# An image network of four layers on one core: the last queries' features in parts behind the key products, keys' values in two banks, shared reciprocals, last taps mixed later, lone steps reordered

## The chip, the cores and the metric

The kernel runs on one core of a Trainium2 chip, in one launch, all in fp32. The metric is the device time of one execution in microseconds (us). Before the change three executions took 2716.63, 2718.47 and 2719.44 us; the median, 2718.47 us, is the time before.

A core has a matrix engine (TensorE, PE in the profile; its weight loads are PEld), a vector engine (VectorE, DVE), a scalar engine (ScalarE, ACT), a general one (GpSimd, POOL) and queues for transfers (SP issues them here). [...] this kernel makes three buffers of two banks ("pair") and two single banks[...]. [...]

## The reference, cut to what matters

x has the shape (4, 512, 64, 64): four images, 512 channels, 4096 pixels. Four layers follow each other, image by image.

```python
# layer 0: attention over the pixels, 64 features
attn = softmax(einsum('bdk,bdq->bkq', key_, query), axis=1)
x = scale * einsum('oc,bchw->bohw', w_out, value @ attn) + x
# layer 1: three convolutions (1x1, 3x3, 1x1); kernels mixed from 8 experts by
# rw = sigmoid(mean over pixels of x @ router_w.T + router_b)
x = relu(bn(conv3(relu(bn(conv2(relu(bn(conv1(x)))))))) + x)
# layer 2: linear attention
Q, K = softplus(Wq x + bq), softplus(Wk x + bk)      # 64 features each
V = Wv x + bv
KV = einsum('bmn,bcn->bmc', K, V)
norm = 1.0 / einsum('bnm,bm->bn', Q, K.sum(-1) + EPS)
x = x + gamma * einsum('bnm,bmc,bn->bcn', Q, KV, norm)
# layer 3: a gate of discounted sums along the columns and then the rows
g = w_proj x + b_proj                                # 1024 channels: gates and sums
x = x + gamma * g[:512] * sigmoid(ds_cumsum_rows(ds_cumsum_columns(g[512:])))
```

## The kernel before, as far as the change touches it

An image is held in four tiles `xs[pr]` of 1024 pixels ("pairs" of two 512-pixel blocks). The order on TensorE is that of the program. `manual_schedule(DVE)` fixes VectorE's order too; elsewhere the order on VectorE and ScalarE is chosen when the program is built.

```python
def pair_psum(name):
    return ps.tile([P, 2, NB], F32, tag="s", name=name, bufs=3)
def bank(name, shape=(P, NB)):
    return ps.tile(list(shape), F32, tag="acc", name=name)
# ... cut ...
def four(name):
    return fourp.tile([P, 2, NB], F32, tag="four", name=name)
# ... cut ...
def mix_by_expert(wc, rw, experts):
    _, j, n, ex = experts
    to = wc[:, j:j + n, :]
    nc.vector.tensor_scalar(to, ex[:, :, 0, :], rw[:, 0:1], None, ALU.mult)
    for e in range(1, E):
        nc.vector.scalar_tensor_tensor(to, ex[:, :, e, :], rw[:, e:e + 1], to, ALU.mult, ALU.add)
```

The end of layer 0: the residual sums of the last two pairs, with the mixing of the experts' kernels (`mix`: on TensorE; `mix_by_expert`: on VectorE, for the last three taps).

```python
for m in range(2, KC):
    out_before(m)
ys = [out_product(pr, m) for m in range(3)]
add_out(pr, 0, ys[0])
mix(wcq, sel, ex0)
ys.append(out_product(pr, 3))
for m in range(1, KC):
    add_out(pr, m, ys[m])
for m in range(KC):
    xm = xs[pr - 1][:, m, :]
    nc.vector.tensor_tensor(xm, xm, flat(ring[8 + m]), ALU.add)
sum_range(pr)
# ... cut ...
mix(wc, sel, ex4)
mix(wc, sel, ex7)
mix_by_expert(wc, rw, ex10)
```

Layer 2: features (two softplus halves per pair of pairs), transposes of the keys and of x, and the sum of key products `g`, which is folded and multiplied with the value weights instead of making V.

```python
def softplus(w, pair, z):
    i = 2 * (len(kts) // 2 % 2)
    e, u = sp[:, i], sp[:, i + 1]
    pos, ln = four(f"pos_{b}_{w}_{pair[0]}"), four(f"ln_{b}_{w}_{pair[0]}")
    nc.scalar.activation(e, z, AF.Abs, bias=col(BQ2 + w))
    nc.scalar.activation(pos, z, AF.Relu, bias=col(BQ2 + w))
    nc.scalar.activation(e, e, AF.Exp, scale=-1.0)
    nc.vector.tensor_scalar(u, e, 1.0, None, ALU.add)
    nc.scalar.activation(ln, u, AF.Ln)
    return lambda: softplus_end(w, pair, e, u, pos, ln)
def softplus_end(w, pair, e, u, pos, ln):
    nc.vector.scalar_tensor_tensor(u, u, -1.0, e, ALU.add, ALU.subtract)
    nc.vector.tensor_tensor(pos, pos, ln, ALU.add)
    for i, pr in enumerate(pair):
        if w:
            k = block(f"k_{b}_{pr}")
            nc.vector.scalar_tensor_tensor(k, pos[:, i, :], 1.0, u[:, i, :], ALU.mult, ALU.subtract,
                                           accum_out=ks[:, pr:pr + 1])
            kts[w, pr] = k
        else:
            nc.vector.tensor_tensor(qs[:, pr, :], pos[:, i, :], u[:, i, :], ALU.subtract)
            kts[w, pr] = None
# ... cut ...
def move(pr, j):
    xtr = pair_psum(f"xtr_{b}_{pr}_{j}")
    for h in range(2):
        n0 = h * NB + j * P
        for kc in range(KC):
            nc.tensor.transpose(xtr[:, h, kc * P:(kc + 1) * P], xs[pr][:, kc, n0:n0 + P], ident)
    xt = four(f"xt_{b}_{pr}_{j}")
    (nc.scalar.copy if j % 2 or (pr > 1 and j) else nc.vector.tensor_copy)(xt, xtr)
    moved.append(xt)
# ... cut ...
h2[2] = conv2(2)
conv3(1, h2[1])
h2[3] = conv2(3)
weights = load_quarters(b)
features(1, (0, 1))()()
conv3(2, h2[2])
rest = features(0, (0, 1))
with tc.manual_schedule(engines={mybir.EngineType.DVE}):
    key_transpose((0, 1))
    rest()()
for step in ahead(0):
    step()
conv3(3, h2[3])
products(0, ahead(1))
weights[2]()
features(1, (2, 3))()()
products(1, ahead(2))
rest = features(0, (2, 3))
# ... cut ...
def normed(pr, between=None):
    den = bank(f"den2_{b}_{pr}")
    nc.tensor.matmul(den, kbd, qs[:, pr, :], start=True, stop=True)
    nrm = block(f"nrm_{b}_{pr}")
    nc.vector.reciprocal(nrm, den)
    if between:
        between()
    nc.vector.tensor_tensor(qs[:, pr, :], qs[:, pr, :], nrm, ALU.mult)
# ... cut ...
def value_product(pr, m):
    y = pair_psum(f"wv_{b}_{pr}_{m}")
    for h in range(2):
        r = slice(h * D, (h + 1) * D)
        nc.tensor.matmul(y[:, h, :], kv[r, m * P:(m + 1) * P], qs[r, pr, :], start=True, stop=True)
    return y
def value_add(pr, m, y):
    xm = xs[pr][:, m, :]
    nc.vector.tensor_tensor(xm, flat(y), xm, ALU.add)
return value_product, value_add, weights, wcq
```

Layer 3: each block takes seven products (a saving of one in eight against the plain form) for two channel groups of a pair. `s` steps make the sums, `g` steps the gates of the block before, `l` the scans of the block before, `y` and `a` a value product of layer 2 and its addition to x. `x` is one single bank of a block, `zy` one pair.

```python
def product(self, k):
    if k == 1:
        self.x = bank(f"sx_{self.name}")
        self.zy = pair_psum(f"zy_{self.name}")
    y = self.x if k in (1, 6, 7, 4) else self.zy[:, 0 if k == 2 else 1, :]
    w, v = weights[k], others[self.pr][k]
    for c in range(2):
        nc.tensor.matmul(y, w[:, c, self.kind, self.j * P:(self.j + 1) * P], v[:, c, :],
                         start=c == 0 and k in (1, 5), stop=c == 1,
                         skip_group_check=k not in (1, 5))
def seed(self):
    nc.scalar.copy(self.zy[:, 0, :], self.x)
def copy_out(self, k):
    self.e[k] = block(f"e{k}_{self.name}")
    nc.scalar.activation(self.e[k], self.x, AF.Identity, bias=self.bias[k - 2])
# ... cut ...
tiles = [(pr, (pr + j) % 2) for pr in range(NPAIR) for j in range(2)]
units = {}
steps = (("s1", "s seed", "l rows 1"), ("g1", "g seed", "y", "l rows 0", "l turn 1"),
         ("s5", "l turn 0", "a"), ("g5", "l columns 1"),
# ... cut ...
last_steps = (("g1", "g seed", "l rows 1", "l rows 0"), ("g5",), ("g6", "g copy_out 2", "l turn 1"), ("g2",),
              ("g7", "g copy_out 3", "l columns 1", "g fourth", "l turn 0", "l columns 0", "l sigmoid 1",
               "l sigmoid 0"), ("g4",), ("g3", "g third", "g first", "g second"))
# ... cut ...
with tc.manual_schedule(engines={mybir.EngineType.DVE, mybir.EngineType.Activation}):
    for m in range(KC):
        value_add(0, m, value_product(0, m))
        if m == 1:
            sum_x(0, 0)
    for part in range(1, 4):
        sum_x(0, part)
# ... cut ...
for i in range(len(tiles) + 1):
    who = {"l": last, "s": Sums(1, i) if i < len(tiles) else None, "g": Gates(0, i - 1) if i else None}
    made = None
    for step in steps if who["s"] else last_steps:
        for what in step:
            name, *args = what.split()
```

## Time and profile before

| what | before |
|---|---|
| time, median of 3 | 2718.47 us |
| span of the profiled execution | 2717.1 us |
| TensorE busy | 2667.3 us (98%) |
| VectorE busy | 1961.2 us (72%) |
| ScalarE busy | 1306.6 us (48%) |
| moved by DMA | 115.15 MB, mean 42 GB/s |
| reciprocals of layer 2 (VectorE, 128 x 512) | 16, 3356 ns each |
| clock granted to TensorE | 0.997 |

Busy time is a union of instructions[...]. [...] A wait in the profile is idle time of an engine, with the instruction whose end released it. Line numbers (L588) are those of the kernel before.

### The profile page before, as it was taken

To read this page: it belongs to the slowest core of one execution; us is meant where nothing else is said; L and a number is where in the kernel's file an instruction comes from. 1 tells how busy PE (TensorE), PEld (TensorE's weight loads), DVE (VectorE), ACT (ScalarE), POOL (GpSimd) and SP (SyncE) were. 2 spreads that over 40 slices of the span, in tenths; PEclk is the share of its full clock that TensorE was granted. 3 is DMA by queue.
4 is the path that set the end of the run, shared out by engine and by line. 5 is a ranking of instruction groups with operands and counts; after the bars stand their busy time and mean duration, and the time that the engine had idled before them with its cause. 6 is when DMAs were issued, how large, how long until landed. Compare 5 with 4: busy or idle time off the path is not lost.

```text
span 2717.1 us, 25649 instructions
## 1 busy us (share of the span) xinstructions
PE 2667.3 (98%) x10046; PEld 1114.7 (41%) x10046; DVE 1961.2 (72%) x2197; ACT 1306.6 (48%) x1483; POOL 10.7 (0%) x26
## 2 busy tenths in 40 slices
PE   8999999999999999999999999999999999999998
PEld 3333364344333345444433334544443333554443
DVE  2688766787468876678747778667874777866787
ACT  4544354445555535345555453535555555352545
POOL 1000000000000000000000000000000000000000
PEclk9999999999999999999999999999999999999999
DMA  5000200021200020002220002001121000200011
GB/s 188 1 1 0 101 31 1 16 108 74 82 1 1 1 101 31 1 24 101 78 78 1 1 1 101 32 0 60 64 108 47 1 1 1 101 31 1 31 47 48
DMA packets 34545, 115.15 MB, mean 42 GB/s; under 512 B 2928, under 2 KB 12144, under 8 KB 32880
## 3 DMA queue, kind: packets, MB, share of 16 engines
q1 hardware_dynamic: 34416, 113.43, 11.1%
q8 instruction: 81, 1.33, 0.2%
q14 instruction: 48, 0.39, 0.0%
HBM read 79.86 MB, written 33.55 MB: 42 GB/s over the span
## 4 chain that ended last, share of the span: by engine, by line
PE 86%; DVE 9%; ACT 2%; DMA 1%; issue 1%; SPq 1%; DVEq 0%; ACTq 0%
PE s L248 17%; PE av L263 17%; PE sx L769 14%; PE zy L769 11%; PE c L444 4%; PE kq L209 4%; PE c L493 3%; PE c L516 2%; PE z L543 2%; PE wv L687 2%; PE vv L209 2%; PE g L605 2%; PE xtr L588 2%; PE c2e L493 2%; PE y L307 1%
## 5 line engine op out<-in xcount | busy, mean ns | idle before, releaser
L248 PE MATMUL s<-qv,key 64*128 64x512 f32 x2048 | 469.1, 603 | 1.8 <-ACT ring L251 1.8
L256 DVE TENSOR_TENSOR acc<-acc,ring 128x1024 f32<-128x1024 f32 x312 | 381.7, 1223 | 100.7 <-ACT ring L251 71.9
L251 ACT ACTIVATE ring<-s 128x1024 f32<-128x1024 f32 x336 | 317.7, 1038 | 224.1 <-PE s L248 224.0
L263 PE MATMUL av<-ring,qv 128*64 128x512 f32 x1344 | 304.5, 595 | 0.0
L248 PEld LDWEIGHTS s<-qv,key 64*128 64x128 f32 x2048 | 189.4, 187 | 274.8 <-issue 173.2
L256 DVE TENSOR_TENSOR acc<-acc,ringx 128x1024 f32<-128x1024 f32 x168 | 205.5, 1223 | 102.8 <-ACT ringx L251 90.2
L251 ACT ACTIVATE ringx<-s 128x1024 f32<-128x1024 f32 x176 | 172.1, 1040 | 207.0 <-PE s L248 207.0
L769 PE MATMUL sx<-t,sx 128*128 128x512 f32 x512 | 236.9, 597 | 0.0
L263 PEld LDWEIGHTS av<-ring,qv 128*64 128x64 f32 x1344 | 93.3, 137 | 198.6 <-issue 198.6
L263 PE MATMUL av<-ringx,qv 128*64 128x512 f32 x704 | 167.2, 598 | 0.0
L774 ACT COPY zy<-sx 128x512 f32<-128x512 f32 x64 | 36.5, 570 | 240.1 <-PE sx L769 230.6
L819 DVE TENSOR_TENSOR_SCAN t<-sx,t 128x512 f32<-128x512 f32 x128 | 148.8, 1210 | 1.7
L769 PEld LDWEIGHTS sx<-t,sx 128*128 128x128 f32 x512 | 95.9, 190 | 127.8 <-issue 121.1
L808 ACT COPY t<-s 128x1024 f32<-128x1024 f32 x64 | 127.2, 1994 | 40.5 <-DVE s L802 40.5
L778 ACT ACTIVATE e<-sx,prm_sb 128x512 f32<-128x512 f32 x128 | 86.9, 686 | 123.8 <-PE sx L769 123.8
L802 DVE TENSOR_TENSOR_SCAN s<-wc,s 128x512 f32<-128x512 f32 x128 | 146.0, 1204 | 0.0
L825 ACT ACTIVATE s<-t 128x1024 f32<-128x1024 f32 x64 | 125.5, 1987 | 1.0 <-DVE t L819 0.9
L769 PE MATMUL sx<-t,wq 128*128 128x512 f32 x256 | 117.0, 598 | 7.5 <-ACT e L778 7.5
L209 PE MATMUL kq<-x,wqkv_sb 128*64 128x512 f32 x512 | 116.2, 607 | 6.3 <-DMA x<-in_x_dram 5.6
L769 PE MATMUL zy<-t,wq 128*128 128x512 f32 x256 | 118.7, 604 | 2.5 <-ACT zy L774 2.5
L769 PE MATMUL zy<-x,wq 128*128 128x512 f32 x256 | 116.2, 594 | 0.0
L769 PE MATMUL sx<-x,wq 128*128 128x512 f32 x256 | 116.2, 594 | 0.0
(195 smaller groups left out, 3390.0 us busy)
## 6 DMA issues: line engine op xcount, KB each, us to landing
out_dram<-s SPq DMA_DIRECT2D x64, 512.0 KB, 2.6
x<-in_x_dram SPq DMA_DIRECT2D x15, 2048.0 KB, 8.5
ex<-in_packed_dram SPq DMA_DIRECT2D x8, 1536.0 KB, 6.3
ex<-in_packed_dram SPq DMA_DIRECT2D x4, 2048.0 KB, 7.9
ex<-in_experts_dram SPq DMA_DIRECT2D x4, 2048.0 KB, 7.9
wq<-in_wproj_t_dram SPq DMA_DIRECT2D x32, 256.0 KB, 4.5
ex<-in_experts_dram SPq DMA_DIRECT2D x4, 1536.0 KB, 7.1
x<-in_x_dram SPq DMA_DIRECT2D x4, 512.0 KB, 6.3
```

The lines of the kernel that those rows point to most:

```text
L209: nc.tensor.matmul(y[h * D:(h + 1) * D, :], wqkv_sb[:, kc, col0:col0 + D], xs[pr][:, kc, h * NB:(h + 1) * NB], start=kc == 0, stop=kc == K ...
L248: nc.tensor.matmul(s[:, h, :], key[r, kt * P:(kt + 1) * P], qry[r, pr * NB:(pr + 1) * NB], start=True, stop=True)
L251: nc.scalar.activation(p, s, AF.Exp)
L256: nc.vector.tensor_tensor(accs[pr], accs[pr], p, ALU.add)
L263: nc.tensor.matmul(avs[pr][h * D:(h + 1) * D, :], vt[:, kt, :], ring[i % RING][:, h, :], start=kt == 0, stop=kt == NT - 1)
L444: nc.tensor.matmul(y[:, h, :], wc[:, kc, :], xs[pr][:, kc, h * NB:(h + 1) * NB], start=kc == 0, stop=kc == KC - 1)
L493: nc.tensor.matmul(y[:, lo - a:hi - a], u, v[:, lo:hi], start=dy == 1, stop=dy == 2)
L769: nc.tensor.matmul(y, w[:, c, self.kind, self.j * P:(self.j + 1) * P], v[:, c, :], start=c == 0 and k in (1, 5), stop=c == 1, skip_group_c ...
L802: nc.vector.tensor_tensor_scan(self.half(i, h), along[:, self.j + 2 * i, :], self.half(i, h), 0.0, ALU.mult, ALU.add)
L808: nc.scalar.copy(self.t[i].rearrange("p (w r) -> p w r", w=W), self.s[i].rearrange("p (r w) -> p w r", w=W))
L819: nc.vector.tensor_tensor_scan(th, down[:, i, :], th, 0.0, ALU.mult, ALU.add)
L825: nc.scalar.activation(self.s[i].rearrange("p (r w) -> p w r", w=W), tw, AF.Sigmoid)
```

## The change

It has five parts. The features of the last two pairs' queries leave the middle of layer 2: their products come in four parts, behind the key products, between the folding steps and the value products, and in the first block of layer 3; their softplus and division follow in the first two blocks. The product of keys and values goes into two single banks of 256 columns. The denominators of two pairs are made with 16 equal columns per head instead of 64, so that two pairs share one reciprocal of 64 rows, and a small product (`spread`) sends the inverse back to all rows. The last taps are mixed behind the last residual sums. And single steps change their order: the second transpose of x goes through single banks, transposes and key products alternate in twos instead of ones, VectorE's order is fixed in the whole middle of layer 2, and the first and last block of layer 3 have orders of their own.

```diff
+    kbd = const.tile([P, 32], F32, tag="kbd", name="kbd")
     nc.gpsimd.memset(kbd, 0.0)
+    spread = const.tile([P, P], F32, tag="spread", name="spread")
+    for h in range(2):
+        nc.vector.tensor_reduce(spread[:, h * D:h * D + 1], ident.rearrange("p (q i) -> p i q", i=32)[:, 16 * h:16 * h + 1, :],
+                                AX.X, ALU.add)
+        nc.vector.tensor_scalar(spread[:, h * D:(h + 1) * D], ones[:, 0:D], spread[:, h * D:h * D + 1], None, ALU.mult)
... cut ...
             for m in range(1, KC):
                 add_out(pr, m, ys[m])
+            mix_by_expert(wcq, rw, ex10)
             for m in range(KC):
... cut ...
         mix(wc, sel, ex7)
-        mix_by_expert(wc, rw, ex10)
... cut ...
+        def move_by_halves(pr, j):
+
+            xt = four(f"xt_{b}_{pr}_{j}")
+            for h in range(2):
+                n0 = h * NB + j * P
+                xtr = bank(f"xtr_{b}_{pr}_{j}_{h}")
+                for kc in range(KC):
+                    nc.tensor.transpose(xtr[:, kc * P:(kc + 1) * P], xs[pr][:, kc, n0:n0 + P], ident)
+                nc.scalar.copy(xt[:, h, :], xtr)
+            moved.append(xt)
... cut ...
         def products(pr, between=()):
-            between = list(between)
-            for j in range(TPB):
-                t = pr * TPB + j
-                if j + 2 < TPB:
-                    move(pr, j + 2)
-                elif between:
-                    between.pop(0)()
-                xt = moved.pop(0)
-                for h in range(2):
-                    nc.tensor.matmul(g[h * D:(h + 1) * D, :], kts[pr][:, j, h * D:(h + 1) * D], xt[:, h, :],
-                                     start=t == 0, stop=t == NPAIR * TPB - 1)
+            for j0 in range(0, TPB, 2):
+                for step in [lambda j=j: move(pr, j) for j in (2, 3)] if j0 == 0 else between:
+                    step()
+                for j in range(j0, j0 + 2):
+                    t = pr * TPB + j
+                    xt = moved.pop(0)
+                    for h in range(2):
+                        nc.tensor.matmul(g[h * D:(h + 1) * D, :], kts[pr][:, j, h * D:(h + 1) * D], xt[:, h, :],
+                                         start=t == 0, stop=t == NPAIR * TPB - 1)
... cut ...
+        def invert(pair):
+            den = bank(f"den2_{b}_{pair[0]}")
+            for i, pr in enumerate(pair):
+                nc.tensor.matmul(den[32 * i:32 * (i + 1), :], kbd, qs[:, pr, :], start=True, stop=True,
+                                 tile_position=(0, 32 * i))
+            inv = block(f"inv_{b}_{pair[0]}")
+            nc.vector.reciprocal(inv[0:D, :], den[0:D, :])
+            return inv
+
+        def divide(pair, inv):
+            nrm = pair_psum(f"nrm_{b}_{pair[0]}")
+            for i, pr in enumerate(pair):
+                r = slice(32 * i, 32 * (i + 1))
+                nc.tensor.matmul(nrm[:, i, :], spread[r, :], inv[r, :], start=True, stop=True,
+                                 tile_position=(32 * i, 0))
+            q = qs[:, pair[0]:pair[1] + 1, :]
+            nc.vector.tensor_tensor(q, q, nrm, ALU.mult)
... cut ...
-            rest()()
-        for step in ahead(0):
-            step()
-        conv3(3, h2[3])
-        products(0, ahead(1))
-        weights[2]()
-        features(1, (2, 3))()()
-        products(1, ahead(2))
-        rest = features(0, (2, 3))
... cut ...
-        with tc.manual_schedule(engines={mybir.EngineType.DVE}):
+            rest = rest()
+            move(0, 0)
+            move_by_halves(0, 1)
+            conv3(3, h2[3])
+            g = bank(f"g_{b}", (P, C))
+            keys = features(1, (2, 3))
+            rest()
+            keys = keys()
+            products(0, ahead(1))
+            keys()
+            products(1, ahead(2))
... cut ...
-                nc.vector.tensor_scalar(kbd[r, r], ones[r, 0:D], ksum[r, :], 1e-6, ALU.mult, ALU.add)
+                nc.vector.tensor_scalar(kbd[r, 16 * h:16 * (h + 1)], ones[r, 0:16], ksum[r, :], 1e-6, ALU.mult, ALU.add)
             key_transpose((2, 3))
-            rest = rest()
-            normed(0)
-            rest()
-        products(2, ahead(3))
-
-        normed(1)
-        products(3, [lambda: normed(2)])
-        g_sb = block(f"gsb_{b}", (P, C))
-        nc.scalar.copy(g_sb, g)
... cut ...
-        def make_kv():
+            inv = invert((0, 1))
+            products(2, ahead(3))
+            divide((0, 1), inv)
+            weights[2]()
+            products(3)
+            g_sb = block(f"gsb_{b}", (P, C))
+            nc.scalar.copy(g_sb, g)
+            gt = block(f"gt_{b}", (P, KC, P))
+
+            late = (0, (2, 3), pair_psum(f"z_{b}_0_2"))
+            feature_part(*late, 0, 0, 2)
... cut ...
+            gk = pair_psum(f"gk_{b}")
             for kc in range(KC):
-                nc.tensor.matmul(kvp, gt[:, kc, :], wv_sb[:, kc, :], start=kc == 0, stop=kc == KC - 1)
-            nc.vector.scalar_tensor_tensor(kv, bv_sb, ksum, kvp, ALU.mult, ALU.add)
... cut ...
-        with tc.manual_schedule(engines={mybir.EngineType.DVE}):
-            normed(3, make_kv)
+                nc.tensor.matmul(gk[:, 0, kc * P:(kc + 1) * P], g_sb[:, kc * P:(kc + 1) * P], fold,
... cut ...
+            nc.scalar.copy(gt, gk[:, 0, :].rearrange("p (kc c) -> p kc c", c=P))
+            feature_part(*late, 0, 2, 2)
+            kv = small.tile([P, C], F32, tag="kv", name=f"kv_{b}", bufs=1)
+            for i in range(2):
+                part = slice(i * C // 2, (i + 1) * C // 2)
+                kvp = bank(f"kvp_{b}_{i}", (P, C // 2))
+                for kc in range(KC):
+                    nc.tensor.matmul(kvp, gt[:, kc, :], wv_sb[:, kc, part], start=kc == 0, stop=kc == KC - 1)
+                nc.vector.scalar_tensor_tensor(kv[:, part], bv_sb[:, part], ksum, kvp, ALU.mult, ALU.add)
+
+
+        left = [lambda: feature_part(*late, 1, 0, 2), lambda: feature_part(*late, 1, 2, 2),
+                lambda: left.append(softplus(*late)), lambda: left.pop()(),
+                lambda: left.append(invert((2, 3))), lambda: divide((2, 3), left.pop())]
... cut ...
             def product(self, k):
-                if k == 1:
+                if self.x is None:
... cut ...
         steps = (("s1", "s seed", "l rows 1"), ("g1", "g seed", "y", "l rows 0", "l turn 1"),
... cut ...
-        last_steps = (("g1", "g seed", "l rows 1", "l rows 0"), ("g5",), ("g6", "g copy_out 2", "l turn 1"), ("g2",),
+        first_steps = (("s1", "s seed", "q"), ("s5", "q"), ("s6", "s copy_out 2"), ("s2", "s first", "q"),
+                       ("s7", "s copy_out 3", "s fourth", "y"), ("s4", "s third", "a", "d"), ("y", "a", "q"),
+                       ("s3", "s second"))
+        last_steps = (("g5", "l rows 1", "l rows 0"), ("g1", "g seed"), ("g6", "g copy_out 2", "l turn 1"), ("g2",),
                       ("g7", "g copy_out 3", "l columns 1", "g fourth", "l turn 0", "l columns 0", "l sigmoid 1",
                        "l sigmoid 0"), ("g4",), ("g3", "g third", "g first", "g second"))
... cut ...
             for part in range(1, 4):
                 sum_x(0, part)
... cut ...
+                                left.pop(0)()
                         elif name == "t":
                             if i % 2 and i // 2 + 1 < NPAIR:
```

## The prediction

> **What bounds the kernel now.** I read the page first. TensorE's matmul row is busy for nearly the whole span:
>
> ```profile
> PE 2667.3 (98%) x10046; PEld 1114.7 (41%) x10046; DVE 1961.2 (72%) x2197; ACT 1306.6 (48%) x1483; POOL 10.7 (0%) x26
> ```
>
> VectorE (72%) and ScalarE (48%) have room on average, DMA is at 42 GB/s. So time falls only if TensorE gets fewer instructions, waits less, or wastes less between instructions. The waits of TensorE come second; the columns are the total, the number and the longest in us:
>
> ```profile
> PE sx L769 <- ACT e L778: 7.5, 12, 0.8
> ...
> PE xtr L588 <- ACT pos L552: 3.9, 4, 1.1
> PE wv L687 <- DVE kv L678: 3.7, 4, 0.9
> ...
> PE gk L668 <- ACT gsb L664: 2.7, 4, 0.7
> PE zy L769 <- ACT zy L774: 2.5, 4, 0.7
> PE y L307 <- DVE x L312: 2.4, 4, 0.6
> ...
> PE xtr L588 <- DVE x L518: 1.6, 4, 0.4
> PE wv L687 <- DVE x L692: 1.5, 4, 0.4
> ```
>
> Almost each comes four times, once per image. All recorded TensorE idle time is 2717.1 - 2667.3 = 50 us, so even a perfect removal is under 2%. Third, the timeline of TensorE in layer 2 of image 0 (start, duration, engine, line; an idle time and its releaser in brackets):
>
> ```profile
> 417.86 1.09 PE L588 MATMUL xtr<-ident,x 128*128 128x128 f32 x8 [0.41 <-DVE x L518]
> 418.88 1.08 PE L605 MATMUL g<-xt,kt 128*64 128x512 f32 x4
> 419.89 1.09 PE L588 MATMUL xtr<-ident,x 128*128 128x128 f32 x8
> ...
> 464.33 1.94 PE L605 MATMUL g<-xt,kt 128*64 128x512 f32 x8
> 466.95 1.16 PE L668 MATMUL gk<-fold,gsb 128*128 128x128 f32 x8 [0.69 <-ACT gsb L664]
> 467.95 1.02 PE L640 MATMUL den<-wc,kbd 128*128 128x512 f32 x2
> 468.88 3.67 PE L677 MATMUL gk<-wv_sb,gt 128*128 128x512 f32 x8
> 473.47 3.71 PE L687 MATMUL wv<-wc,kv 64*128 64x512 f32 x16 [0.92 <-DVE kv L678]
> ```
>
> This shows a cost that no idle row has. A stretch of 4 key products starts 1.01 after the start before it; 8 in a row take 1.94 where 4 take 1.08, so 4 more cost 0.86 and the change of kind costs 0.15. The transposes' 1.02 splits alike (8 further ones come 0.93 later where two groups of transposes follow each other at 406.05 and 406.98). One round trip between the two kinds costs about 0.28, and it is counted as busy.
>
> [...]
>
> **The change part by part**, per image; minus is saved TensorE time.
>
> 1. Taps mixed later. The transfer of the sum vector waits: eight expert mixes run between the router and the first residual add (add at 307.29, although its product was ready near 304.3), and the last output product waits 0.60 for that add. With the mixes behind the adds the first add can start at 304.9. -0.60. The mixes, 8 x 0.61, then end near 315 and the tap sums near 322 instead of 320; they are used at 339.97. Nothing lost.
>
> 2. Second transpose in two single banks instead of a paired buffer: no wait for the softplus. -(1.10+1.10+0.92+0.77)/4 = -0.97. The queries' softplus tail and the four weight sums (1.22 each on VectorE at 394 to 408) no longer stand between the third convolution's adds: its last pass takes 7.82 from 410.04 to the next transpose, where 16 products take 7.02. -0.80. The pass before takes 7.46, 7.71, 7.06, 7.07: -0.27.
>
> 3. Moves and products in twos: two round trips fewer in each of pairs 0 to 2, one in pair 3: 7 x 0.28 = -2.0.
>
> 4. Shared reciprocals. Removed: four 128-column denominators, 0.94 + 0.96 + 1.06 + 0.93 = 3.89. Added: two pairs of 32-column ones, concurrent, 0.96 each, and two pairs of spreads of 32 rows, 0.86 plus about 0.35 for going in and out of another tile shape, 1.2 each: 4.3. +0.43. VectorE loses two of four reciprocals and gets two wide multiplies for four narrow ones: 4 x 3.36 + 4 x 0.69 = 16.2 becomes 2 x 3.36 + 2 x 1.22 = 9.2. Those 7 us lie beside TensorE's work and count only through waits.
>
> 5. Last queries' features in four parts. The same 6.9 us of products moves from 440.89 into the gaps: two parts cover the copies of g and of its folded form (-0.69), two go between the value products (-0.36) and behind the seed. The key-value product in two banks lets VectorE finish half one during half two: -0.92. Each part brings changes of shape: about eight of 0.15 to 0.2 instead of one, +1.05.
>
> 6. First block's order. A value product between the seventh and the fourth product covers the copy of 0.69 that cost 0.78. But the late softplus now sits on ScalarE ahead of the first copy-out: absolute value, relu, exp at 1.0, then 0.69 on VectorE, then log 1.0, about 5.4 us from the end of the features, while TensorE has s5, s6, s2 = 5.2 us: +0.3. Net -0.48.
>
> 7. New waits. (a) The keys' softplus now precedes pair 0's moves in VectorE's fixed order; the copy of transpose 2 ends some 5.5 us after the features, and the fourth move needs its buffer at 4.8: +0.5. (b) The second division sits in block 1 behind s5. Its PSUM pair must be the third one: two are held by the open blocks, the third by a value product whose add comes after four row scans (4.56) on VectorE. Today that add ends at 499.7, just after s5 (499.5); now the scans start later, because the second reciprocal (3.36) starts with s3 (1.72) and the last sum of block 0 follows it: about 1.55 later. +1.8.
>
> 8. Last block: g5 ahead of g1. Today g5 waits 0.66 for the seed's copy; then g6 must, since it adds into the bank that the copy reads. 0.
>
> Sum: -0.60 -0.97 -0.80 -0.27 -2.0 +0.43 -0.69 -0.36 -0.92 +1.05 -0.48 +0.5 +1.8 = -3.3 us. Four images: -13; 2718.5 - 13 = 2705. I lean 1 us lower, as (b) is the least certain positive term.
>
> **The rivals.** *The new waits do not come*: if the buffers are freed sooner than I order them, or the last block's reorder does save 0.66, the gain is 5.5 to 6 us per image, 2695. For: VectorE has 7 us less to do per image, and the parts are spread over the very places that wait today. Against: the scans and the add keep their program order. *The fixed order of VectorE and ScalarE becomes the bound*: the whole middle of layer 2 now has VectorE in program order, and the late softplus puts four ScalarE and five VectorE operations into the block with least slack; each slip of the scans by 1 us stops TensorE for 1 us at the division, and a slip over 5 would reach the sigmoid chain (columns end 504.2, used from 506.8). For: block 1 already waits 0.33 for that chain. Against: VectorE idles 6.80 there now. It would give 2712 to 2722. *Changes of shape eat it*: if each costs 0.3 rather than 0.15, parts 4 and 5 lose 2 us more per image: 2713.
>
> **Range and chances.** The certain terms (1, 2, 3, the covered waits) are -6.6 per image, the certain losses +1.5, the doubtful ones 0 to +3.5 with the rest of 6. That spans -1.6 to -5.7 per image, 2712 to 2696; a little wider for what I have not seen: 2694 to 2714. A gain of 2% (54 us) is beyond all idle time; a loss of 2% needs 13 us per image. So: faster 0.01, same 0.98, slower 0.01.
>
> **What would show it.** Right: no wait of the transposes on `pos`, of `gk` on `gsb`, of `wv` on `kv`, of `y` on `x`; transposes in groups of 16; 8 reciprocals of 64x512 in layer 2; a TensorE wait at the second spread of 1 to 2 us, released by VectorE's `x`; about 0.66 still before g6 of the last block; the gap from image to image (672.6 from the first projection at 688.87 to that at 1361.5) falling to about 669. Wrong: the sum fails if waits of the first block grow over 1 us, if the spreads run one after the other, or if half a `kv` waits for the other half.

## The result and the profile after

The changed kernel takes 2699.82 us (median of six executions, 2697.83 to 2701.86), the kernel before 2718.84 us beside it (six, 2716.63 to 2720.49). The ratio is 0.9931, with a 95% interval from 0.9918 to 0.9944: 19.0 us less. The prediction was 2704.0 with a range of 2694 to 2714, and 0.98 for "within 2%".

The busy row and the chain that ended last, on the page of the kernel after:

```profile
PE 2660.0 (99%) x10110; PEld 1118.1 (41%) x10110; DVE 1938.9 (72%) x2189; ACT 1307.7 (49%) x1487; POOL 10.7 (0%) x26
...
PE 92%; DVE 5%; ACT 3%; issue 1%; DMA 0%; SPq 0%; ACTq 0%; DVEq 0%
```

TensorE has 64 instructions more than before and is busy for 7.3 us less, since fewer changes of kind lie between them (singles, below) and since it worked 3.4 us at a granted clock of 0.50 in image 0 where it was 6.8 us before (last part of the point by point); its idle time fell from 50 to 36 us. Before, the chain had 86% on TensorE and 9% on VectorE. The bound has not moved, the path is only cleaner. The waits of TensorE, complete (total, number, longest, in us):

```profile
PE kq L215 <- DMA x<-in_x_dram: 5.6, 1, 5.6
PE sx L803 <- ACT e L812: 5.2, 12, 0.8
PE nrm L659 <- DVE x L726: 4.7, 4, 1.2
PE wo_t L167 <- DVE wot_sb L165: 3.2, 1, 3.2
PE sx L803 <- ACT zy L808: 2.5, 4, 0.7
PE s L254 <- ACT ring L257: 1.8, 8, 0.2
PE xtr L608 <- DVE xt L610: 0.9, 4, 0.2
```

Gone are the waits on `pos`, `kv` and `gsb`, the one of `y` on `x`, and those of the value products. Two are new, both foretold: `nrm`, the spread of the second division, and `xtr` on `xt`, the buffer of pair 0. The timeline of TensorE in layer 2 of image 0 (start, duration, line; in brackets idle time and releaser):

```profile
422.81 1.09 PE L608 MATMUL xtr<-ident,x 128*128 128x128 f32 x8
424.14 1.09 PE L608 MATMUL xtr<-ident,x 128*128 128x128 f32 x8 [0.24 <-DVE xt L610]
...
427.03 1.97 PE L608 MATMUL xtr<-ident,x 128*128 128x128 f32 x16
428.92 1.94 PE L623 MATMUL g<-xt,kt 128*64 128x512 f32 x8
...
434.56 0.38 PE L679 MATMUL kfold<-ks,fold 128*128 128x4 f32 x2
...
450.75 1.89 PE L547 MATMUL z<-x,wqk_sb 128*64 128x512 f32 x8
452.57 1.16 PE L700 MATMUL gk<-fold,gsb 128*128 128x128 f32 x8
453.65 1.94 PE L547 MATMUL z<-x,wqk_sb 128*64 128x512 f32 x8
...
491.01 1.13 PE L659 MATMUL nrm<-inv,spread 32*128 32x512 f32 x4 [1.18 <-DVE x L726]
```

The transposes come in 16s and the key products in 8s, where they came in 8s and 4s; `gk` starts without a wait because two parts of the features (`z`) cover the copies around it. The row at 424.14 is the buffer wait: it starts 1.33 after the one before it, where a second group of 8 otherwise starts about 0.9 later.

By stages, from TensorE's first instruction of each (us, mean over the images): layer 0's first output products to the first convolution 13.03 before, 12.36 after; the keys' first features to the key transpose 21.36, 21.10; key transpose to the first value product 67.20, 56.79; from there to the fourth product of block 1 39.92, 46.77. Two of these move against each other since the last features have gone from the one to the other. Together -4.49 per image, 18.0 us in four. The other stages are unchanged within 0.02 in images 1 and 2; in the last image the first projections to the first scores take 43.4 instead of 44.0, since a wait of 0.5 on VectorE's copy `qv` isn't there in the profile after.

Image 0 brought 2.5 us more at the start, which no edit touches; they are told of at the end of the point by point. 18.0, 0.6 and 2.5 make the 21.1 us between the two profiles; the medians lie 19.0 apart.

### The profile page after: what moved, and what is told of

It is laid out like the page before. It is cut to its first block, busy times and chain, and to the rows that moved or that the text cites. A ratio compares the mean times of both kernels' runs of the same rounds, so it can differ in the third digit from the quotient of the medians.

```text
span 2696.0 us, 25777 instructions
## 1 busy us (share of the span) xinstructions
PE 2660.0 (99%) x10110; PEld 1118.1 (41%) x10110; DVE 1938.9 (72%) x2189; ACT 1307.7 (49%) x1487; POOL 10.7 (0%) x26
## 3 DMA queue, kind: packets, MB, share of 16 engines
q8 instruction: 81, 1.33, 0.2%
## 4 chain that ended last, share of the span: by engine, by line
PE 92%; DVE 5%; ACT 3%; issue 1%; DMA 0%; SPq 0%; ACTq 0%; DVEq 0%
PE s L254 17%; PE av L269 17%; PE sx L803 14%; PE zy L803 10%; PE z L547 4%; PE kq L215 4%; PE c L522 4%; PE c L450 4%; PE c L499 3%; PE wv L721 2%; PE y L313 2%; PE vv L215 2%; PE g L623 2%; PE xtr L608 2%; PE c2e L499 2%; DVE s L836 1%
## 5 line engine op out<-in xcount | busy, mean ns | idle before, releaser
L803 PE MATMUL zy<-x,sx 128*128 128x512 f32 x256 | 116.3, 595 | 0.0
```

## The experiments

Each kernel ran beside the kernel before; stage times are from the profiled execution. Theory: the gain is the sum of small terms that the prediction lists, each worth what its waits and changes of kind say. Rivals: waits that disappear from the list only change their name; VectorE's fixed order is a new bound; the changes of kind eat the gain.

| run | us, median | ratio to before, 95% interval |
|---|---|---|
| after | 2699.82 | 0.9931 (0.9918 to 0.9944) |
| singles | 2706.34 | 0.9949 (0.9932 to 0.9965) |
| no_halves | 2704.20 | 0.9942 (0.9925 to 0.9959) |
| early_sums | 2703.78 | 0.9939 (0.9923 to 0.9956) |
| one_kv | 2703.15 | 0.9939 (0.9923 to 0.9956) |
| early_features | 2699.86 | 0.9927 (0.9911 to 0.9944) |
| mix_early | 2702.77 | 0.9941 (0.9921 to 0.9961) |
| split_last | 2699.11 | 0.9927 (0.9911 to 0.9944) |
| own_recip | 2705.38 | 0.9949 (0.9933 to 0.9966) |
| own_recip_y | 2695.32 | 0.9916 (0.9900 to 0.9933) |
| divide_later | 2694.17 | 0.9909 (0.9893 to 0.9926) |
| better | 2690.98 | 0.9898 (0.9881 to 0.9914) |
| better_ok | 2690.71 | 0.9889 (0.9873 to 0.9906) |

The intervals of the totals overlap for neighbours in this table; the verdicts below rest on stage times, which repeat within 0.02 us from image to image, except where numbers of single images are given.

### Moves and products singly again (singles)

```diff
-            for j0 in range(0, TPB, 2):
-                ... two moves, then two key products
+            for j in range(TPB):
+                ... one move, then one key product, as in the kernel before
```

> Changed kernel, but transposes and key products alternate one by one again. Theory (each change of kind costs TensorE time that is counted as busy): 7 round trips per image x 0.28 us come back, less the 0.4 us that pair 0 waits for a buffer in the changed order: +1.6 us per image, +6 us in all, and the stretch of pair 1 grows from 7.5 to 8.0 us with no idle row in it. Rival (the order matters only through waits[...]): 0 to -2 us, stretch of pair 1 at 7.5 us.

Key transpose to first value product: 58.46 against 56.79, +1.67 per image, and no row of the list of waits is new. Pair 1 in image 0 (its first transposes, then the first instruction behind its key products):

```profile
429.33 1.09 PE L608 MATMUL xtr<-ident,x 128*128 128x128 f32 x8
...
437.46 0.39 PE L681 MATMUL kfold<-ks,fold 128*128 128x4 f32 x2
```

These are 8.13 us, and 7.53 in the kernel after (427.03 to 434.56), without an idle time in either; 8.0 and 7.5 were expected. The buffer wait of pair 0 (0.43 by the starts above) is gone with it, so the twos save 2.10 and cost 0.43. This is the largest single term of the change, and it stands in no list of waits: it was TensorE's own busy time.

### The second transpose in a paired buffer again (no_halves)

```diff
-            move_by_halves(0, 1)
+            move(0, 1)
```

> Changed kernel, but the second transpose uses a paired buffer again. Theory A (the buffer alone made the wait): the wait on the softplus of 0.8 to 1.1 us comes back in each image, +4 us. Theory B (half of that wait came from the weight sums, which delayed ScalarE's softplus in the kernel before and are now later): ScalarE has read the features at 404.7 and the transposes could start at 404.2, so a wait of 0.4 to 0.6 us, +2 us in all.

+0.87 per image (57.66). TensorE in image 0:

```profile
406.42 1.04 PE L608 MATMUL xtr<-ident,x 128*128 128x128 f32 x8
407.83 1.09 PE L608 MATMUL xtr<-ident,x 128*128 128x128 f32 x8 [0.38 <-ACT pos L561]
408.76 7.29 PE L522 MATMUL c<-h,wc 128*128 128x512 f32 x16
```

The wait on the softplus returns, but with 0.38 and not with the 0.97 that it had before. So theory B has the wait right, and theory A the total. The rest of the old wait came by way of ScalarE: in image 0 of the kernel before it began this softplus at 406.96, 0.8 after the features' end, behind a copy of the convolution's result at 405.90 that waited for VectorE's add of 404.58, and ahead of that add VectorE had done a weight sum (398.77) and the end of the keys' softplus. Here it begins 0.1 after the features' end. That the sums and not the softplus made the delay was not tested apart. In the kernel after, the second transpose starts 0.88 after the first and the third convolution's pass takes 7.03; here 1.41 and 7.29. The transpose and the pass behind it share the loss.

### The weight sums before the third convolution's last pass again (early_sums)

```diff
         conv3(2, h2[2])
+        weights[2]()
...
             divide((0, 1), inv)
-            weights[2]()
```

> Changed kernel, but the four weight sums stand right behind the third convolution's third pass, where VectorE's order is free. Theory (the sums of 1.22 us each stood between the convolution's adds): the third and last passes grow again by 0.3 and up to 0.9 us and TensorE waits on VectorE's x, +1.5 to +4.5 us in all. Rival (the early tail of the queries' softplus was what delayed the adds, and that stays late): within 0.5 us of the changed kernel.

Key transpose to first value product +0.49 in each image; keys' features to key transpose +0.14, +1.92, +0.34, +0.08. In all 4.4 us, 1.1 per image. The second number is one wait, which came in one image only:

```profile
PE c L522 <- DVE x L524: 1.6, 1, 1.6
```

VectorE in that image shows where it comes from:

```profile
1063.60 1.23 DVE L742 TENSOR_TENSOR sx<-wq 128x1024 f32<-128x1024 f32 x1 [10.07 <-DMA wq<-in_wproj_t_dram]
1064.74 1.28 DVE L524 SCALAR_TENSOR_TENSOR x<-c,bn_s,x 128x1024 f32<-128x1024 f32 x1
```

The add (L524) that frees the convolution's buffer stands behind a weight sum (L742), and this sum waits for the transfer of its weights. So the later place does more than clear the adds: it gives the transfer time. (The kernel before had this wait too, 8.55 us in image 0.) In images 2 and 3 the same sum waits 8.49 and 8.23 us and costs TensorE little. Where these sums stand, the same program text costs between 0.6 and 2.4 us an image.

### The keys' values in one bank again (one_kv)

```diff
-            for i in range(2):
-                part = slice(i * C // 2, (i + 1) * C // 2)
+            for i in range(1):
+                part = slice(0, C)
```

> Changed kernel, but keys times values in one bank of 512 columns with one VectorE operation. Theory (the second bank hides the first half's VectorE step): the first value product waits again about 0.9 us on kv, +3.7 us in all; the product itself takes the same 3.65 us. Rival (the half-width products cost what they save, or the division had made the wait): within 1 us of the changed kernel.

+0.89 per image, all of it one wait that reappears:

```profile
PE wv L721 <- DVE kv L710: 3.4, 4, 0.8
```

### The last features undivided and in front of the key products (early_features)

```diff
+            late = features(0, (2, 3))
             kfold = bank(f"kfold_{b}", (P, NPAIR))
...
+            late = late()
             inv = invert((0, 1))
             products(2, ahead(3))
+            late()
             divide((0, 1), inv)
+            inv = invert((2, 3))
...
-            late = (0, (2, 3), pair_psum(f"z_{b}_0_2"))
-            feature_part(*late, 0, 0, 2)
...
-            feature_part(*late, 0, 2, 2)
+            divide((2, 3), inv)
...
-        left = [ ... parts, softplus, reciprocal, division in the first two blocks of layer 3 ... ]
+        left = []
```

> Changed kernel, but the last queries' features are made whole before the key sums, as in the kernel before, and divided before the keys' values. Theory (their parts fill the waits for the copies of g and of its folded form, and the first block's copy-outs): waits of 0.7 us on gsb, up to 0.9 us on gt and kv, 0.4 us before the third value product come back, less about 0.7 us for fewer changes of shape and the 1.3 us at the second spread: between -1 and +1 us per image, -4 to +4 us in all. Rival (the parts are the gain itself): +6 us or more.

Key transpose to first value product 64.04, +7.25; the stage after it 39.75, -7.02: +0.2 per image, and nothing in the total. Its waits that the kernel after doesn't have:

```profile
PE zy L802 <- ACT zy L807: 2.9, 4, 0.7
PE gk L701 <- ACT gsb L696: 2.7, 4, 0.7
...
PE den L649 <- DVE wc L577: 2.0, 4, 0.5
```

1.9 us of waits per image come back (0.7 of `zy` only because the first block's new order has nothing behind its seed here), and yet the image is only 0.2 longer. What the four parts cover, they cost again: the second division moves with them, and with them absent its wait of 1.18 is gone too, and so are changes of kind. The most laborious part of the change, taken with the division that it carries into layer 3, brings almost nothing. It does pay once that division stands one product later (divide_later, below): 56.79 + 45.52 = 102.31 for the two stages against 103.79 here, and 2694.17 us against 2699.86.

### The taps mixed before the residual adds again (mix_early)

```diff
-            mix_by_expert(wcq, rw, ex10)
...
         mix(wc, sel, ex7)
+        mix_by_expert(wc, rw, ex10)
```

> Changed kernel, but the last taps are mixed where the builder puts them, as in the kernel before. Theory: TensorE waits 0.60 us before the last output product in each image, +0.66 us per image (12.36 back to 13.02 from the first output products to the first convolution), +2.6 us in all. Rival (the later mixing cost its gain elsewhere, in the tap sums): within 1 us of the changed kernel, and the second convolution starts earlier.

Two executions. Layer 0's first output products to the first convolution 13.02 against 12.36: +0.66, and `PE y L313 <- DVE x L318` returns with 2.4 us in four. The convolutions that follow are unchanged, so the later tap sums are in time.

### The last block's products in halves (split_last)

Here the seed (a copy of `x`'s product into the first bank of the pair `zy`) gets the second half of g5 behind it instead of all of g5 in front, and g2 is split around the next copy.

```diff
-        last_steps = (("g5", "l rows 1", "l rows 0"), ("g1", "g seed"), ("g6", "g copy_out 2", "l turn 1"), ("g2",),
-                      ("g7", "g copy_out 3", ...
+        last_steps = (("h 5 0", "l rows 1", "l rows 0"), ("g1", "g seed"), ("h 5 1",), ("g6", "g copy_out 2", "l turn 1"),
+                      ("h 2 0",), ("g7", "g copy_out 3"), ("h 2 1", ...
```

> Changed kernel, and in the last block of each image g5 and g2 are cut in two halves of 0.86 us, one half behind g1 (covers the seed's copy), one behind g7 (covers the third copy-out). Theory (TensorE waits there 0.66 and 0.78 us for ScalarE, and any independent product fills it): both waits gone, -1.4 us per image for the first three and less at the end of the last, -4 to -6 us in all. Rival (the end of the image is set by the scans and sigmoids behind it, not by TensorE): the next image's projections do not start earlier, 0 us.

Fourth product of block 1 to the next image: 175.47, unchanged. The waits only took other names (TensorE, image 0):

```profile
668.10 1.88 PE L803 MATMUL sx<-x,wq 128*128 128x512 f32 x4
670.64 1.13 PE L803 MATMUL zy<-t,wq 128*128 128x512 f32 x2 [0.66 <-ACT zy L808]
...
679.43 1.98 PE L803 MATMUL zy<-x,sx 128*128 128x512 f32 x4 [0.42 <-DVE e L867]
```

The half of g5 at 670.64 writes the second bank of `zy`, the seed the first, and it waits 0.66 us for the seed all the same. This is the rival "a wait changes its name", shown. Whether that wait is the chip's or the program builder's making, this run doesn't tell; better_ok takes the pair apart.

### An own reciprocal for every feature (own_recip)

The shared reciprocals and their spread are undone; the places of the two divisions stay.

```diff
-            den = bank(f"den2_{b}_{pair[0]}")
+            den = pair_psum(f"den2_{b}_{pair[0]}")
-                nc.tensor.matmul(den[32 * i:32 * (i + 1), :], kbd, qs[:, pr, :], ...)
+                nc.tensor.matmul(den[:, i, :], kbd, qs[:, pr, :], start=True, stop=True)
-            nc.vector.reciprocal(inv[0:D, :], den[0:D, :])
+            nc.vector.reciprocal(inv, den)
-            nrm = ...  # the spread, two products
-            nc.vector.tensor_tensor(q, q, nrm, ALU.mult)
+            nc.vector.tensor_tensor(q, q, inv, ALU.mult)
```

> Changed kernel, but without sharing: each pair of pairs gets 128-column denominators in a paired buffer, one reciprocal of 128 x 1024 and the multiply straight from it, no spread product. Theory (TensorE is the bound and VectorE's relief is worth nothing by itself; the spread costs two small products and a wait for a third buffer): VectorE has 6.7 us more per image, TensorE about 0.2 us less, and the wait of 1.2 us at the second spread is gone although the scans start 3.3 us later: -5 us in all against the changed kernel. Rival (the shared reciprocals pay by freeing VectorE): the scans of block 0 end 3.3 us later, the sigmoid chain or the next value product waits for them, +3 to +12 us.

The first stage went as expected: -0.27. The total did not: 2705.38, 5.6 above the kernel after, where a gain was expected. The stage behind it takes 48.54 against 46.77. TensorE and VectorE in image 0:

```profile
490.44 1.44 PE L708 MATMUL wv<-wc,kv 64*128 64x512 f32 x4 [2.04 <-DVE s L818]
```

```profile
483.29 6.56 DVE L644 RECIPROCAL inv<-den 128x1024 f32<-128x1024 f32 x1 [0.68 <-PE den L642]
489.76 0.63 DVE L818 TENSOR_TENSOR s<-zy,e 128x512 f32<-128x512 f32 x1
```

A value product in block 1 wants the paired buffer that block 0's last sum (`s`, L818) frees, and this sum stands behind the reciprocal of 6.56 us. So VectorE, 72% busy, did become the bound, through a buffer. I had left that buffer out.

That wait explains 2.04, and the wider denominators 0.84 (1.82 where two narrow ones take 0.98), but the spread (1.06), its wait (1.18) and its changes of shape are gone from the stage, and still it is 1.77 longer. I put the rest down to the clock. TensorE's stretch with the wait and the one behind it (window, length, busy time and instructions of each engine, granted clock, DMA share, GB/s):

```profile
487.73:491.14 3.41, 1.36 (x6) 0.30 (x4) 3.41 (x3) 0.57 (x1) 0.00 (x0) 1.00 0.00 0
491.15:494.54 3.39, 3.39 (x6) 1.18 (x5) 3.39 (x4) 1.88 (x1) 0.00 (x0) 0.50 0.00 0
```

Behind the idle time of 2.04 us the granted clock is 0.50 for 3.39 us, and so in all four images; half of that time, 1.7 us, is an estimate of what it costs. Behind the 1.18 us wait of the kernel after the clock is 1.00:

```profile
491.10:494.40 3.30, 3.30 (x10) 1.35 (x11) 2.21 (x2) 0.73 (x1) 0.00 (x0) 1.00 0.00 0
```

Four times 1.7 make an estimated 6.8 us of the profiled execution for the clock alone; its mean granted clock was 0.995, that of the kernel after 0.998. Without them own reciprocals would have come out at 2698.6, near the kernel after: sharing them is no gain in itself, it keeps VectorE out of the way. This is worked out; the next run tests it.

### The same with the value product behind the fifth product (own_recip_y)

```diff
+        second_steps = ... # block 1: the value product and its add move from g1 to s5, ahead of the division
```

> The kernel with own reciprocals (128 x 1024, no spread), and in block 1 the first value product stands behind s5 instead of behind g1. Theory (what stopped TensorE for 2.0 us was one buffer: that value product takes the paired buffer that block 0's last sum frees behind the 6.6 us reciprocal): the wait is gone, no other takes its place, 667.66 - 0.27 - 1.3 = 666.1 us from image to image, 2694 us. Rival (VectorE's 3.2 us more are themselves on the path): TensorE waits elsewhere in block 1, on the sigmoids or on an addition, and the distance stays near 669 us.

666.7 to 666.9 us per image (expected 666.1), the kernel after 667.6 to 667.7. The stage fell from 48.54 to 46.09. What is left of the waits:

```profile
PE wv L708 <- DVE x L713: 3.3, 4, 0.8
...
PE wv L708 <- DVE s L818: 1.3, 4, 0.3
```

2.04 of wait became 0.83 + 0.33, and no stretch of layers 2 and 3 up to TensorE's last product has a clock below 1.00: -0.88 of wait and the estimated -1.70 make -2.58, measured -2.45. So the reading of own_recip holds for the larger part: a buffer and then the clock. That no other wait takes its place does not hold: 0.83 us on an addition of VectorE is new, as the rival said of its kind, and it is about what the image is longer than expected; the distance did not stay near 669.

### The second division one product later (divide_later)

```diff
-                 ("s5", "l turn 0", "a", "q"), ("g5", "l columns 1"),
+                 ("s5", "l turn 0", "a"), ("g5", "q", "l columns 1"),
```

> Changed kernel, but the second division stands behind g5 instead of s5 in block 1. Theory (its paired buffer is freed by the addition behind the row scans 1.2 us after s5): g5 covers the wait of 1.72 us, no wait at the spread, -5 us in all. Rival (what was waited for is VectorE itself, and the column scans behind the division then come later): the wait moves to the copy-out in front of s4 in block 1, 0 us.

45.52 against 46.77: -1.25 per image, and no `nrm` in the list of waits. One word in another place is worth more than the shared reciprocals or the late features. 2694.17 us, ahead of both kernels.

### Four edits together (better)

The later division; the keys' softplus between pair 0's moves; two paired buffers for the last block; a value product of block 1 moved between g7 and s4. With the last one pair 1's sums leave out the last value product, which is added after they have been taken: the work is the same, so the time may be read, but this is not the computation of the reference.

```diff
-        def products(pr, between=()):
+        def products(pr, between=(), mid=None):
...
+                first = [lambda: move(pr, 2)] + ([mid] if mid else []) + [lambda: move(pr, 3)]
...
-                y = self.x if k in (1, 6, 7, 4) else self.zy[:, 0 if k == 2 else 1, :]
+                    self.z1 = pair_psum(f"z1_{self.name}")[:, 0, :] if self.alone else self.zy[:, 1, :]
+                y = self.x if k in (1, 6, 7, 4) else self.zy[:, 0, :] if k == 2 else self.z1
```

> Changed kernel with four further edits: the second division behind g5; the second value product of block 1 between g7 and s4; the keys' softplus between the third and fourth transposes of pair 0; and in the last block two paired buffers, one for each accumulator, with g5 whole behind g1 and g2 in halves behind g6 and g7. Theory: 1.25 + 0.33 + 0.43 + 1.44 us per image, the last term not or hardly in the last image, whose end is set by the scans: -12 us in all against the changed kernel, 2687 to 2689. The last block shows no wait of TensorE on the seed (with one paired buffer it waited although g5 writes the other bank). Rival (TensorE's waits of the last block are only moved to the next image's first projection, as with the halves alone): -8 us, 2692.

The softplus between the moves: 56.33, -0.45, which is the buffer wait of pair 0. First value product to block 1's fourth: 44.92, -1.85. Last block to the next image: 174.51, -0.96, where -1.44 (both waits of 0.66 and 0.78) was expected. And none of that is kept: the next image's projections now wait, for the copy `qv` of VectorE. From them to the first scores images 1 to 3 take 44.29, 45.03 and 47.04 instead of 43.42, 6.1 us in all, where three times 0.96 and 0.20 in the last image had been saved. The rival (waits moved to the next image) is nearer than the theory, whose 2687 to 2689 us were not reached.

### The three that leave nothing out (better_ok)

> Three of the four edits of the run that reached 2690.98 us, without the moved value product, so that nothing is left out: the second division behind g5 in place of s5, the keys' softplus between the moves of pair 0, two paired buffers in the last block. Sum of parts: from that run's 2690.98 add back what the moved value product brought (its stage was 44.92 against 45.52 with the later division alone, 0.60 per image, 2.4 us): 2693.4. If the last block's two buffers bring nothing in all, because the next image's first projections then wait for VectorE's copy of its features (L236) as long as was saved, the same sum comes from the later division (2694.17) and the 0.45 per image of the keys' softplus: 2692.4. The two theories lie 1 us apart and the total cannot tell them apart; the stages can: first value product to s4 of block 1 45.5, first key transpose to first value product 56.3, s4 to the next image 174.5, and kq to s 44.3 to 47.0 as in that run.

2690.71 us (2688.71 to 2693.09). The stages are 56.33, 45.53 and 173.84: the last block saves 1.64 per image, more than expected. Its g1 and g5 in image 0 have no wait any more now that their banks belong to two pairs:

```profile
667.39 1.88 PE L805 MATMUL sx<-x,wq 128*128 128x512 f32 x4
669.11 1.88 PE L805 MATMUL z<-t,wq 128*128 128x512 f32 x4
```

But the projections of the next image take 44.52, 46.98 and 44.67 where they took 43.42:

```profile
PE kq L215 <- DVE qv L236: 4.0, 3, 1.8
```

3 x 1.64 + 0.86 (last image, up to the end of the span) = 5.8 us saved, 1.10 + 3.56 + 1.25 = 5.9 us given back. So the second theory on record holds for this execution: the last block's buffers bring nothing in all. The engine named is not the cause. VectorE had been idle for 10.91 us before the copy in question, released by ScalarE's copies of the keys, and ScalarE made these late:

```profile
1360.73 1.06 ACT L331 ACTIVATE junk<-x 128x1024 f32<-128x1024 f32 x1 [5.14 <-DMA x<-in_x_dram]
...
1364.28 1.06 ACT L331 ACTIVATE junk<-x 128x1024 f32<-128x1024 f32 x1
...
1365.44 2.36 ACT L235 COPY key<-kq 64x512 f32<-64x512 f32 x4
```

Four sums over the next image's x (`junk`, about 1.2 us each with the reading of the sum) stand ahead of the keys; in the kernel after only two do, and the keys' copies start 7.67 us after their projections' start instead of 9.73. The order on ScalarE is chosen when the program is built, and these edits changed it elsewhere; the later division alone does not (43.4 in divide_later). An order of ScalarE held fixed there should keep the 1.64; it wasn't tried. The 3.56 contains the clock again: the wait before image 2's third group of projections was 1.80 us, and behind it the granted clock is 0.50 (first line), while behind the 1.04 us wait of image 1 it is 1.00:

```profile
1369.10:1372.10 3.00, 3.00 (x10) 0.97 (x8) 0.61 (x2) 0.00 (x0) 0.00 (x0) 0.50 0.03 5
...
702.80:705.80 3.00, 3.00 (x16) 1.01 (x14) 0.67 (x2) 0.00 (x0) 0.00 (x0) 1.00 0.00 0
```

The parts that are kept, 1.25 and 0.45 per image, make 2699.8 - 6.8 = 2693. The median is 2.3 lower, and the four executions lie in two groups, 2688.7 and 2688.8, 2692.6 and 2693.1; the profiled one is the 2693.09. The mean clock of each is on record: 0.997 in the profiled one, 0.998 in the other three. So one stretch more at 0.50 fits the 2693.1, but this clock doesn't part 2692.6 from the lower two, and what makes that execution longer stays open. Against divide_later (0.9893 to 0.9926) the intervals overlap, and their order isn't settled. Every execution of either (2688.7 to 2695.3) is shorter than every one of the kernel after (2697.8 to 2701.9), though the ratio's interval of divide_later still overlaps that of the kernel after; its stage times decide.

## Why the prediction was right, point by point

| step | predicted, us per image | measured | from |
|---|---|---|---|
| 1 taps mixed later | -0.60 | -0.66 | mix_early |
| 2 second transpose in single banks | -0.97 | -0.87 | no_halves |
| 2 weight sums away (-0.80 - 0.27) | -1.07 | -1.10 | early_sums, 4.4 / 4 |
| 3 moves and products in twos | -2.0 | -2.10 | singles, 1.67 + 0.43 |
| 4 shared reciprocals | +0.43 | +0.19 | rows: 4.08 for 3.89 |
| 5 late features, waits covered (-0.69 - 0.36) | -1.05 | -1.05 | those rows are gone |
| 5 late features, changes of shape | +1.05 | +0.71 | what is left of the sum; +1.05 with step 2 by rows, see below |
| 5 two banks for `kv` | -0.92 | -0.89 | one_kv |
| 6 first block's order | -0.48 | -0.40 | timeline |
| 7a buffer of pair 0 | +0.5 | +0.43 | timeline; gone in singles |
| 7b wait at the second spread | +1.8 | +1.25 | divide_later |
| 8 last block | 0 | 0 | timeline |
| sum | -3.3 | -4.49 | the stages |

The measured terms come from different runs and from rows, and all but one stand by themselves; the changes of shape of step 5 are only the remainder. The mechanism was right in all parts. Two sizes were clearly too high, 7b by 0.55 and the reciprocals by 0.24. The whole difference is 1.2 per image, 4.7 us: the sum of the prediction, 2705.3, becomes 2700.6, beside the measured 2699.8. The leaning of 1 us went the right way and was too small. The distance from image to image, foretold as about 669, is 667.7.

**Step 2 agrees in part by luck.** The two undone edits give 0.87 and 1.10, but they don't stand for the kernel before. There the stretch from the key transpose to the end of the third convolution's last pass took 11.69 (mean; in image 0 from 406.05 to the transposes of 417.86), in the kernel after

```profile
402.38 1.09 PE L584 MATMUL ktr<-ident,k 128*128 128x128 f32 x8
...
412.02 7.09 PE L547 MATMUL z<-x,wqk_sb 128*64 128x512 f32 x32
```

9.64, so -2.05, while no_halves and early_sums bring back 0.87 and 0.49 of it. In the stage ahead early_sums adds 0.62, most of it the one wait of image 1, where only 0.26 had been gained. By rows step 2 is thus -2.31 for the predicted -2.04, and the remainder of step 5 becomes 1.05, as predicted. Both edits undone together would settle it; this wasn't run. So it is not shown that the changes of shape were sized too high.

**7b was mis-sized**, 1.25 for 1.8. I let the row scans start 1.55 later and added the old slack of 0.2. On VectorE in the kernel after:

```profile
481.49 3.34 DVE L652 RECIPROCAL inv<-den 64x512 f32<-64x512 f32 x1
484.75 0.62 DVE L831 TENSOR_TENSOR s<-zy,e 128x512 f32<-128x512 f32 x1
485.30 4.55 DVE L836 TENSOR_TENSOR_SCAN s<-wc,s 128x512 f32<-128x512 f32 x4
489.77 1.19 DVE L726 TENSOR_TENSOR x<-wv,x 128x1024 f32<-128x1024 f32 x1
```

Reciprocal, last sum, four scans, add: exactly the chain of step 7b, and the spread starts when the add ends. From the start of s3 (481.21 on TensorE) to the add's end are 9.75 us; TensorE's own work from there to the end of s5 (489.84) is 8.63. The difference, 1.1, is the wait. I had taken the old order's slack of 0.2 and added a delay to it; the two lengths, both to be had from rows of before, would have been the better way.

**The changes of shape in steps 4 and 5.** The two narrow denominators of two pairs took 0.98 from start to start and their two spreads 1.06, the latter predicted at 1.2. That such narrow products run side by side was an estimate from rows of before: 16 mixes with 32 columns (L187) took 1.93 us where 32 products with 64 columns (L543) took 7.04, and four instructions with 64 rows (L687) 1.13 where four with 128 rows (L769) took 1.88; with 32 rows it had none. The first rival (no new waits) is refuted by the rows of `nrm` and `xtr`, the third (0.3 for each change) by the measured costs of both steps, 0.9 or 1.2 per image by the two countings, where it needs about 3.5.

**The second rival**, VectorE's order as the bound, was given no weight beyond 7b, and in the kernel as built it has none. own_recip shows how near it lies: with 6.56 us in one piece in place of 3.34 it takes over.

**The start of image 0.** Of the profile's 2.5 us there the prediction says nothing. 1.0 of them lie in the first projections: the same 32 instructions take 10.20 us before and 9.16 after, since those that start before 11 us (before) and before 8 us (after) take 1.06 to 1.12 us each and the later ones 0.59. What makes the early ones longer isn't shown; the profile gives a granted clock of 1.00 there (0 to 14 us) in both. 1.5 lie behind an idle time of 3.19 us before `wo_t`, which both kernels have (3.18 after; first line before, second after):

```profile
62.90:69.90 7.00, 6.98 (x22) 4.11 (x24) 1.74 (x3) 2.05 (x2) 0.00 (x0) 0.52 0.00 0
```

```profile
62.00:69.00 7.00, 7.00 (x30) 3.54 (x31) 3.23 (x4) 3.66 (x4) 0.00 (x0) 0.76 0.00 0
```

The kernel before works 6.8 us at a granted clock of 0.50, the kernel after 3.4; half of the difference, 1.7 us, is an estimate of what that is worth at most. The twelve other profiles have the one or the other with the same code there, so it comes from the execution and not from the edits.

## What to carry to other kernels

When the busy row of the bound engine says 98%, compare the starts of like rows before counting waits: the largest term here was the change between two kinds of small matmuls (2.10 us per image), which no wait shows, and doing them two at a time was the cheapest edit. The wait of 1.18 us that went through a rotating buffer stood there although VectorE's reciprocal had become shorter (3.34 us for two pairs, own ones 6.56); find who frees such a buffer and put the consumer one product later, which is worth trying first since it costs a word (1.25 us per image in divide_later). And look at the clock behind every idle time of TensorE that is longer than the others: inside layers the granted clock stayed at 1.00 behind those of 0.9 to 1.65 us, and behind the six of 1.80 to 2.05 us it was 0.50 for 3.4 us, by the estimate above 1.7 us more.

## What the runs showed of the hardware that I had not expected

- **A granted clock of 0.50 behind short idle times.** All six idle times of 1.80 to 2.05 us inside layers (four in own_recip, one of 1.86 in better, one of 1.80 in better_ok) were followed by 3.4 us at a granted clock of 0.50; none of 0.9 to 1.65 us was (1.54 in better, 1.65 in early_sums, the four of 1.18 in the kernel after). The stretch behind the 1.65 us of early_sums:

```profile
1066.10:1069.10 3.00, 3.00 (x10) 1.14 (x12) 3.00 (x4) 3.00 (x3) 0.00 (x0) 1.00 0.00 0
```

  The four of own_recip stand at the same place of each image, so the six count as three cases. At the start of image 0 the clock behind the 3.19 us was 0.50 for 3.4 us in five profiles and for 6.8 us in nine. What sets the clock isn't shown.
- **The reciprocal of half the partitions took nearly as long**: 64x512 3.34 us, 128x512 3.36; 128x1024 took 6.56.
- **A product waited for a copy into the other bank of its paired buffer**: TensorE 0.66 us for ScalarE's write in split_last; in two buffers the wait is gone (better_ok). Whether the chip or the program's building makes this wait isn't shown.
- **Products of 32 rows overlapped**: two spreads of 32x512 (four instructions, 0.64 us each by the median) took 1.13 us, as the two halves of a value product with 64 rows each did; four instructions of the full 128 rows took 1.88.
